# A gated cross-attention and expert layer: the router's logits computed as extra columns of the projection

## The chip, the cores and the metric

The kernel runs on one core of one Trainium2 chip. TensorE (PE) multiplies matrices, VectorE (DVE) and ScalarE (ACT) do elementwise work, GpSimd (POOL) does small operations and issues the indirect transfers, SyncE (SP) issues most of the plain ones. The metric is the device time of one execution in microseconds, the median of several runs. All data are float32.

## The reference

A cross-attention of 4096 rows on 3202 context rows, gated by a tanh and added to x; then a layer norm, a router with eight experts (two per row, at most 640 rows per expert), and the experts' two matrix products, gated and added again.

```python
def xattn(encoder_hc, decoder_hq, w_sim, b_sim, W_qv, b_qv):      # (4096, 512), (3202, 512)
    w1, w2, w3 = w_sim[:d], w_sim[d:2*d], w_sim[2*d:]
    Sim = (encoder_hc @ w1)[:, :, None] + (decoder_hq @ w2)[:, None, :] \
        + einsum('bid,bjd->bij', encoder_hc * w3, decoder_hq) + b_sim[0]
    A = softmax(Sim, axis=2)
    hq_hat = einsum('bij,bjd->bid', A, decoder_hq)
    Batt = softmax(max(Sim, axis=2), axis=1)
    hc_bar = einsum('bi,bid->bd', Batt, encoder_hc)[:, None, :]
    hc_hat = broadcast_to(hc_bar, encoder_hc.shape)
    feats = concatenate([encoder_hc, hq_hat, encoder_hc * hq_hat, encoder_hc * hc_hat], axis=-1)
    return feats @ W_qv + b_qv                                    # W_qv (2048, 512)

def ffn(xf, w_router, b_router, w1, b1, w2, b2):                  # E = 8 experts, top 2, FF = 2048
    logits = xf @ w_router + b_router
    gates = softmax(logits, axis=-1)
    topv, topi = top_k(gates, 2)
    cap = int(1.25 * n / e)                                       # 640 slots per expert
    ...
    h = gelu(einsum('ecd,edf->ecf', buf, w1) + b1[:, None, :])
    out = einsum('ecf,efd->ecd', h, w2) + b2[:, None, :]
    ...

x = x + tanh(g_xattn[0]) * xattn(layernorm(x), ctx_1024, ...)
x = x + tanh(g_ffn[0]) * ffn(layernorm(x), ...)
```

Two facts of this computation matter for the change. The logits are a product of the normed row with the router: with mean m and standard deviation s of a row x1, ((x1 - m) / s) @ w_router equals (x1 @ C) / s, where C is w_router with each column's mean taken away, since a constant row times C gives zero. And x1 itself is a sum of x, a bias and products with the four blocks of W_qv, so x1 @ C can be had by multiplying the same factors with (block @ C).

## The kernel before

The kernel has three stages.

Stage 1 (L112 to L720) works through the 4096 rows in eight groups of 512. `stage_s` computes the scores of a group against all context rows; `stage_e` subtracts each row's maximum (L433), exponentiates on ScalarE (L434) and sums; `stage_v` multiplies by the context's values (L493) and forms the factors of the projection. `stage_d` (L616 to L672) of the group before follows `stage_s`: it multiplies hq_hat and x * hq_hat with the second and third block of W_qv. Each of these products is done with seven half-size products in place of eight, from sums and differences of the quarters (names such as A11, S1, p6, u2, u3 are those of that scheme). In `stage_d` a product `prod` (L631) has two row blocks of 128 by four contraction chunks, each a matmul with 256 columns, and both row blocks share one PSUM bank; VectorE sums them (L646, L656, L660), scales by 1/sum and adds x and the bias (L642), and the rows go to DRAM as `r_d` (L672). A ring of six PSUM banks (`ps_m`) serves scores, values and projection.

Group 0 differs: it also builds what the later groups read. `build` (L251) makes the combined keys, `build_values` (L284) and `build_weights` (L288 to L301) the combined values and the combined projection weights, which go through the double-buffered tiles vc and vs to the DRAM tensors kt_d, vs_d and wt_d. The maximum of group 0 passes through transposes (mps, L405) and a product with ones (mbps) before `stage_e`, and the values products of group 0 are the plain ones (vv).

Stage 2 (L738 to L953) goes over the rows again, in tiles of 128. Its steps hold four tiles (seven steps) or two (the last two). For every tile, `tile_mm` (L780) multiplies q with the weights W1 + hc * W4 (x1p, L792; four matmuls of 512 columns), adds r (L796) to get x1, stores it to `out` (L797), and takes its statistics (L799, L800). `norms` (L803) computes rstd on GpSimd (L806, L807) and the normed rows xn on VectorE (L810). `tile_tr` (L814) transposes xn with four matmuls against the identity (helper line L99) and copies them to SBUF on ScalarE (L817); `tile_logits` (L820) multiplies with the router in four matmuls of 8 columns and adds its bias (L824). `route` (L826) does the top 2 on small VectorE operations, counts slots with two matmuls against a triangle and ones (L881, L882), and `slots` writes weights (L902), token number (L906) and slot (L916) behind each normed row. `dispatch` (L921) then scatters a step's rows to their experts' buffer `buf_d` with two indirect transfers per tile, issued by GpSimd (L924). The tile xn has three buffers, so that step k writes into what the scatters of step k - 3 read.

The loop at the end of stage 2 sets the order: step g's `tile_mm` and `norms`, then the scatters of step g - 2 with `slots`, then transposes, logits and routing of step g - 1. A scheduler then moves instructions that are ready on each engine. The loads of q (q2T, L784), of r (L789) and of the first expert's weights (L731, L733) are on SP's queue; those weights are placed after the q2T loads of groups 1 and 3.

Stage 3 (L961 to L1176) runs the experts. Its first load from buf_d (xb, L1027) needs all scatters.

Of the kernel before, what the change touches and what calls it, by code (L numbers as in the profile page):

```python
# [14 lines left out]
P = 128  # L15
# [5 lines left out]
def gated_layer(ctx, tc, x, x_t, ctxt, ctxt_t, g_xattn, g_ffn, w_sim, w_sim1, b_sim, W_qv, b_qv, w_router, b_router, w1, b1, w2, b2, out):  # L21
# [13 lines left out]
    TG = 4 * P  # L35
    NG = N // TG
# [24 lines left out]
    tgx = const.tile([P, 1], F32, name="tgx")  # L61
    nc.scalar.activation(tgx, gx, AF.Tanh)
    tgf = const.tile([P, 1], F32, name="tgf")
# [3 lines left out]
    r_d = [dram.tile([P, D], F32, name=f"r_d{t}", tag=f"r_d{t}") for t in range(NT)]  # L67
# [8 lines left out]
    tok_i = const.tile([P, NT], I32, name="tok_i")  # L76
# [3 lines left out]
    sno_i = const.tile([P, E * NST], I32, name="sno_i")  # L80
    nc.gpsimd.iota(sno_i, pattern=[[P, E * NST]], base=0, channel_multiplier=1)
    sno = const.tile([P, E * NST], F32, name="sno")
    nc.vector.tensor_copy(sno, sno_i)

    def layernorm(sm, dst, src, t):
        st = sm.tile([P, 6], F32, name=f"st{t}", tag="st")
        nc.vector.bn_stats(st, src)
        mv = sm.tile([P, 2], F32, name=f"mv{t}", tag="mv")
        nc.vector.bn_aggr(mv, st)
        rstd = sm.tile([P, 1], F32, name=f"rstd{t}", tag="rstd")  # L90
        nc.gpsimd.tensor_scalar(rstd, mv[:, 1:2], EPS, None, ALU.add)
        nc.gpsimd.tensor_tensor(rstd, rstd, neghalf, ALU.pow)
        return nc.vector.tensor_scalar(dst, src, mv[:, 0:1], rstd, ALU.subtract, ALU.mult)
# [18 lines left out]
    with ExitStack() as s1:  # L112
# [16 lines left out]
        wt_d = dram.tile([P, 4, DC, 256], F32, name="wt_d", tag="wt_d")  # L129
# [6 lines left out]
        def diag_rows(dst, name, col):  # L136

            dg = sb.tile([P, 4, P], F32, name=f"dg{name}", tag="dg")
            tt(dg, ident.unsqueeze(1).to_broadcast([P, 4, P]), col.unsqueeze(2).to_broadcast([P, 4, P]), ALU.mult)
            nc.tensor.matmul(dst, ones, dg.rearrange("p a b -> p (a b)"), start=True, stop=True)  # L140
# [51 lines left out]
        def stage_a_rest(qs):  # L192
# [4 lines left out]
            ts(bqv, bqv, tgx, None, ALU.mult)  # L197

        def stage_n(g):
# [16 lines left out]
            nc.gpsimd.tensor_scalar(mr[:, 1, :], mv[:, :, 1], EPS, None, ALU.add)  # L216
            nc.gpsimd.tensor_tensor(mr[:, 1, :], mr[:, 1, :], neghalf.to_broadcast([P, 4]), ALU.pow)
            nc.gpsimd.tensor_copy(mr[:, 0, :], mv[:, :, 0])
            nc.gpsimd.dma_start(mr_d[g].rearrange("k i p -> p k i"), mr)
            nc.gpsimd.dma_start(mrb, row_of(mr_d[g]))  # L220
            for i, q in enumerate(qs):
# [66 lines left out]
        def build_weights(c):  # L288


            vc = sb.tile([P, 2, D], F32, name=f"wc{c}", tag="vc", bufs=2)
            for h in range(2):
                with tc.issue_after(queue[-1].ins):
                    nc.sync.dma_start(vc[:, h, :], W_qv[(h + 1) * D + c * P : (h + 1) * D + (c + 1) * P, :])
            B11, B12, B21, B22 = (vc[:, h, k : k + 256] for h in range(2) for k in (0, 256))
            wt = sb.tile([P, 4, 256], F32, name=f"wt{c}", tag="vs", bufs=2)
# [4 lines left out]
            nc.scalar.dma_start(wt_d[:, :, c, :], wt)  # L301
# [59 lines left out]
        def stage_s(g):  # L361
# [8 lines left out]
            for jj, js in enumerate(PAIRS):  # L370
# [29 lines left out]
                else:  # L400
                    for h in (1, 0):
                        tt(m, m, e[:w, :, h], ALU.max)  # L402
            ps = ps_tr.tile([P, 4, P], F32, name=f"mps{g}", tag="tr")
            for i in range(4):
                nc.tensor.transpose(ps[:, i, :], M[:, i // 2, 0, (i % 2) * P : (i % 2 + 1) * P], ident)  # L405
# [3 lines left out]
            diag_rows(ps, f"m{g}", mt)  # L409
# [11 lines left out]
            live[g]["mt"], live[g]["mb"] = mt, mb  # L421

# [58 lines left out]
        def stage_v(g, early, between):  # L481
# [17 lines left out]
            if g == 0:  # L499
                for i in range(2):  # L500
# [86 lines left out]
            v["x"] = []  # L587
            for i in range(4):
                t = 4 * g + i
                xr = sb.tile([P, D], F32, name=f"xr{t}", tag="xr", bufs=4)  # L590
                with tc.issue_after(queue[-1].ins):
                    nc.sync.dma_start(xr, x[t * P : (t + 1) * P, :])
                with tc.issue_after(v["last"].ins):
                    tt(xr, xr, bqv, ALU.add)
                v["x"].append(xr)
# [20 lines left out]
        def stage_d(g):  # L616
            v = live.pop(g)
            A, xs, ri = v["A"], v["x"], v["ri"]

            def prod(ps, p, start=True, stop=True):  # L620
                wt = st.tile([P, DC, 256], F32, name=f"wp{g}_{p}", tag="st")
                natural = {"1": (0, 0), "2": (1, 0), "3": (1, 256)}
                if p in natural:
                    h, c = natural[p]
                    src = W_qv[(h + 1) * D : (h + 2) * D, c : c + 256].rearrange("(k p) d -> p k d", p=P)
                else:
                    src = wt_d[:, {"5": 0, "6": 1, "7": 2, "4": 3}[p], :, :]
                nc.sync.dma_start(wt, src)
                for m in range(2):
                    for k in range(DC):  # L630
                        nc.tensor.matmul(  # L631
                            ps[:, m, :], A[p][:, k, m * P : (m + 1) * P], wt[:, k, :],
                            start=start and m == 0 and k == 0, stop=stop and k == DC - 1, skip_group_check=True,
                        )

            def tmp(k):
                return sb.tile([P, 2, 256], F32, name=f"{k}d{g}", tag=k)

            def out(c, i, j):
                for m in range(2):  # L640
                    r = xs[2 * i + m][:, j * 256 : (j + 1) * 256]
                    stt(r, c[:, m, :], ri[:, 2 * i + m : 2 * i + m + 1], r, ALU.mult, ALU.add)  # L642

            def out_sum(ps, u, i, j):
                c = tmp("p1")
                tt(c, ps, u, ALU.add)  # L646
                out(c, i, j)

            pa = bank(f"pad{g}")
            prod(pa, "1", stop=False)  # L650
            p1 = tmp("p1")
            nc.scalar.copy(p1, pa)
            p6 = bank(f"p6d{g}")
            prod(p6, "6")
            u2 = tmp("u2")
            tt(u2, p6, p1, ALU.add)  # L656
            p7 = bank(f"p7d{g}")
            prod(p7, "7")
            u3 = tmp("u3")
            tt(u3, p7, u2, ALU.add)  # L660
            pb = bank(f"pbd{g}")
# [4 lines left out]
            p4 = bank(f"p4d{g}")  # L666
# [4 lines left out]
            for i in range(4):  # L671
                nc.sync.dma_start(r_d[4 * g + i], xs[i])  # L672


        zero = kv.tile([P, R], F32, name="zero")
        nc.gpsimd.memset(zero, 0.0)
        nc.gpsimd.memset(zero[:, D + 2 : D + 3], float(4 * N))
# [4 lines left out]
        for g in range(NG):  # L682
# [9 lines left out]
            def between():  # L692
# [6 lines left out]
                if g:  # L699
                    for _ in range(-(-E * NST // (NG - 1))):  # L700
                        if blocks:
                            i = blocks.pop()
                            with tc.issue_after(queue[-1].ins):
                                nc.sync.dma_start(buf_d[i * P : (i + 1) * P, :], zero)
# [9 lines left out]
        hs = sm.tile([P, NG, DC + 1], F32, name="hs", tag="hs", bufs=1)  # L714
# [23 lines left out]
    with ExitStack() as s2:  # L738
# [4 lines left out]
        ps_tr = s2.enter_context(tc.tile_pool(name="ps_tr2", bufs=2, space=PSUM, reuse_waits="tile"))  # L743
        ps_lg = s2.enter_context(tc.tile_pool(name="ps_lg", bufs=2, space=PSUM, reuse_waits="tile"))
        ps_po = s2.enter_context(tc.tile_pool(name="ps_po", bufs=1, space=PSUM, reuse_waits="tile"))

        W1 = c2.tile([P, DC, D], F32, name="W1")
        W4 = c2.tile([P, DC, D], F32, name="W4")
        nc.sync.dma_start(W1, W_qv[0:D, :].rearrange("(c p) d -> p c d", p=P))
        nc.sync.dma_start(W4, W_qv[3 * D : 4 * D, :].rearrange("(c p) d -> p c d", p=P))  # L750
        for c in range(DC):
            nc.vector.scalar_tensor_tensor(
                W1[:, c, :], W4[:, c, :], hc[:, c : c + 1], W1[:, c, :], ALU.mult, ALU.add
            )
        wr = c2.tile([P, DC, E], F32, name="wr")
        nc.sync.dma_start(wr, w_router.rearrange("(c p) e -> p c e", p=P))
# [12 lines left out]
        st2 = {}  # L769
# [10 lines left out]
        def tile_mm(t, mv):  # L780
            g, i = divmod(t, 4)
            if g not in qTs:
                qTs[g] = sb.tile([P, DC, TG], F32, name=f"q2T{g}", tag="q2T")
                ld = nc.sync.dma_start(qTs[g], qT_d[g])  # L784
                if g in (1, 3):
                    with tc.issue_after(ld.ins):
                        load_half(0, g // 2)
            r = sb.tile([P, D], F32, name=f"r2_{t}", tag="r2")
            nc.sync.dma_start(r, r_d[t])  # L789
            ps = ps_mm.tile([P, D], F32, name=f"x1p{t}", tag="mm")  # L790
            for c in range(DC):
                nc.tensor.matmul(  # L792
                    ps, qTs[g][:, c, i * P : (i + 1) * P], W1[:, c, :], start=(c == 0), stop=(c == DC - 1)
                )
            x1 = sb.tile([P, D], F32, name=f"x1_{t}", tag="x1", bufs=G + 2)
            nc.vector.scalar_tensor_tensor(x1, ps, tgx, r, ALU.mult, ALU.add)  # L796
            nc.scalar.dma_start(out[t * P : (t + 1) * P, :], x1)  # L797
            st = sm.tile([P, 6], F32, name=f"st{t}", tag="st")
            nc.vector.bn_stats(st, x1)  # L799
            nc.vector.bn_aggr(mv[:, t - STEPS[step_of[t]][0], :], st)  # L800
            return x1

        def norms(k, x1s, mv):  # L803
# [3 lines left out]
            nc.gpsimd.tensor_tensor(rstd, rstd, neghalf.to_broadcast([P, n]), ALU.pow)  # L807
            xg[k] = sb.tile([P, G, R], F32, name=f"xn{k}", tag="xn")
            for i, x1 in enumerate(x1s):
                nc.vector.tensor_scalar(  # L810
                    xg[k][:, i, :D], x1, mv[:, i, 0:1], rstd[:, i : i + 1], ALU.subtract, ALU.mult
                )

        def tile_tr(t):  # L814
            ps = transposed(ps_tr, xg[step_of[t]][:, t - STEPS[step_of[t]][0], :D], f"xps{t}")
            xT = sb.tile([P, DC, P], F32, name=f"xT{t}", tag="xT")
            nc.scalar.copy(xT, ps)  # L817
            st2[t] = xT

        def tile_logits(t, lg):  # L820
            ps = ps_lg.tile([P, E], F32, name=f"lgp{t}", tag="lg")
            for c in range(DC):
                nc.tensor.matmul(ps, st2[t][:, c, :], wr[:, c, :], start=(c == 0), stop=(c == DC - 1))
            nc.vector.tensor_tensor(lg[:, t - STEPS[step_of[t]][0], :], ps, br, ALU.add)  # L824
# [112 lines left out]
        half_routed = None  # L937
        for g in range(len(STEPS) + 1):
            if g < len(STEPS):
                mv = sm.tile([P, G, 2], F32, name=f"mv{g}", tag="mv")  # L940
                norms(g, [tile_mm(t, mv) for t in STEPS[g]], mv)
            if half_routed is not None:
                dispatch(g - 2, half_routed())
            if g >= 1:
                lg = sm.tile([P, G, E], F32, name=f"lg{g}", tag="lg", bufs=2)
                tiles = STEPS[g - 1]
                for i, t in enumerate(tiles):
# [282 lines left out]
```

## Time and profile before

| | us |
|---|---|
| three runs | 2739.01, 2740.75, 2742.1 (median 2740.75) |
| the profiled execution | 2740.97 |
| its span in the profile | 2739.2 |
| end of the last projection product of stage 1 | 1515.2 |
| first matmul of x1p | 1519.63 |
| first scatter of steps 0, 1, 2, 3, 4 | 1578.0, 1603.7, 1626.0, 1648.3, 1671.1 |
| last scatter's end | 1725.9 |
| first product of an expert | 1734.0 |

The span runs from the first to the last instruction of one profiled execution, and 1.8 us lie around it. The granted TensorE clock was 0.986 on average.

A row of a group of instructions reads: line, engine, operation, output <- inputs, shapes, count; then the busy time and the mean length of one in ns; then the idle time of the engine just before these instructions and what ended it. One float32 matmul appears as two instructions of TensorE. In a row of the timeline, the start and the length in us come first, and the brackets hold the idle time before it and its releaser.

### The profile page before, as it was taken

How to read it: one execution, taken by the hardware profiler on the slowest of the kernel's cores; microseconds unless marked ns; L12 is line 12 of the kernel's file. 1: busy time of each engine (PE TensorE's matmuls, PEld its weight loads, DVE VectorE, ACT ScalarE, POOL GpSimd, SP SyncE). 2: the span in 40 equal slices, each digit the busy share in tenths (PEclk: the TensorE clock that was granted, in tenths of full speed). 3: DMA queues.
4: the chain of work that ended last, by engine and by line, in shares of the span. 5: the costliest groups of instructions: out<-in, count | busy, mean ns of one | idle time of the engine just before them, and what ended most of it. 6: DMA issues, size and time to landing. Idle time of an engine off the chain costs nothing. (4 is left out here: it accounts for less than half of the span.)

```text
span 2739.2 us, 29771 instructions
## 1 busy us (share of the span) xinstructions
PE 2662.6 (97%) x11368; PEld 2101.5 (77%) x11368; DVE 1694.0 (62%) x3318; ACT 412.5 (15%) x665; POOL 218.5 (8%) x257
## 2 busy tenths in 40 slices
PE   8999999999999999999999997799999999999998
PEld 7548888888888888888888554477777777777776
DVE  7765946847558468376583556655747465755654
ACT  1200201202002012021020011111111211111111
POOL 0100000000000000000000045201010010101010
PEclk9999999999999999999999998899999999999999
DMA  7786646646656467466454863222233231423210
GB/s 281 196 294 177 216 158 175 233 162 165 228 161 217 166 167 232 155 171 226 154 187 144 317 230 109 91 77 100 93 118 110 81 123 63 152 81 105 81 58 20
DMA packets 183234, 429.54 MB, mean 157 GB/s; under 512 B 17607, under 2 KB 80320, under 8 KB 181044
## 3 DMA queue, kind: packets, MB, share of 16 engines
q1 hardware_dynamic: 152226, 353.64, 39.9%
q0 software_dynamic: 13648, 36.55, 4.0%
q10 hardware_dynamic: 17217, 37.44, 3.6%
q8 instruction: 90, 1.47, 0.2%
q14 instruction: 53, 0.43, 0.0%
HBM read 351.43 MB, written 83.30 MB: 159 GB/s over the span
## 5 line engine op out<-in xcount | busy, mean ns | idle before, releaser
L384 PE MATMUL pas<-Qp,kt 128*128 128x256 f32 (+1 forms) x728 | 174.6, 381 | 1.2 <-ACT p1s L341 1.2
L994 PE MATMUL pah<-bT,w 128*128 128x320 f32 x512 | 159.0, 433 | 0.9 <-DVE cf L1040 0.8
L493 PE MATMUL pbv<-E,vt 128*128 128x256 f32 (+1 forms) x728 | 159.5, 379 | 0.0
L384 PEld LDWEIGHTS pas<-Qp,kt 128*128 128x128 f32 (+1 forms) x728 | 135.6, 187 | 22.8 <-ACT p1s L341 1.6
L493 PEld LDWEIGHTS pbv<-E,vt 128*128 128x128 f32 (+1 forms) x728 | 138.3, 190 | 18.8
L434 ACT ACTIVATE E<-E 128x1024 f32<-128x1024 f32 (+1 forms) x112 | 110.7, 995 | 167.6 <-DVE E L433 166.2
L433 DVE TENSOR_TENSOR E<-E,mb 128x1024 f32<-128x1024 f32 (+1 forms) x112 | 125.4, 1139 | 12.4 <-ACT mb L420 12.4
L994 PEld LDWEIGHTS pah<-bT,w 128*128 128x128 f32 x512 | 97.1, 190 | 39.9 <-DVE bT L1035 1.2
L792 PE MATMUL x1p<-W,q2T 128*128 128x512 f32 x256 | 122.6, 627 | 4.4 <-DMA q2T<-qT_d 4.4
L994 PE MATMUL pao<-w,h 128*128 128x256 f32 x512 | 121.0, 379 | 0.0
L1146 PE MATMUL op<-w,h 128*128 128x512 f32 x256 | 113.6, 592 | 0.0
L402 DVE TENSOR_TENSOR M<-M,E 128x1024 f32<-128x1024 f32 (+1 forms) x96 | 109.0, 1135 | 6.4
L1169 POOL DMA_INDIRECT out<-acc,ti x40 | 42.8, 1071 | 854.5 <-DVE acc L1168 854.2
L994 PEld LDWEIGHTS pao<-w,h 128*128 128x128 f32 x512 | 96.8, 190 | 16.6 <-issue 4.3
L341 ACT COPY p1s<-pas 128x512 f32<-128x512 f32 (+1 forms) x56 | 31.1, 555 | 488.3 <-issue 257.0
L357 DVE TENSOR_TENSOR E<-p4s,u3s 128x512 f32<-128x512 f32 (+1 forms) x56 | 36.5, 651 | 106.8 <-PE p4s L384 106.8
L792 PEld LDWEIGHTS x1p<-W,q2T 128*128 128x128 f32 x256 | 49.2, 201 | 56.8 <-issue 56.8
L384 PE MATMUL pbs<-Qp,kt 128*128 128x256 f32 (+1 forms) x364 | 88.5, 385 | 4.0 <-DVE E L352 4.0
L445 DVE TENSOR_TENSOR SM<-SM,E 128x1024 f32<-128x1024 f32 (+1 forms) x80 | 88.6, 1107 | 0.0
L1146 PEld LDWEIGHTS op<-w,h 128*128 128x128 f32 x256 | 47.2, 190 | 52.0 <-issue 46.4
L384 PE MATMUL pbs<-q,kt 128*128 128x256 f32 (+1 forms) x364 | 86.6, 379 | 0.0
L384 PE MATMUL p6s<-q,kt 128*128 128x256 f32 (+1 forms) x364 | 86.6, 379 | 0.0
(390 smaller groups left out, 5253.0 us busy)
## 6 DMA issues: line engine op xcount, KB each, us to landing
kt<-kt_d SPq DMA_DIRECT2D x84, 896.0 KB
w<-in_w SPq DMA_DIRECT2D x32, 2048.0 KB
vt<-vs_d SPq DMA_DIRECT2D x28, 896.0 KB
vt<-vs_d SPq DMA_DIRECT2D x28, 640.0 KB
wp<-wt_d SPq DMA_DIRECT2D x32, 512.0 KB
wp<-in_W_qv SPq DMA_DIRECT2D x24, 512.0 KB
kt_d<-ktb ACTq DMA_DIRECT2D x12, 896.0 KB
buf_d<-zero SPq DMA_DIRECT2D x40, 258.0 KB
```

The lines of the kernel that those rows point to most:

```text
L341: nc.scalar.copy(p1, cut(pa))
L357: tt(done(1, 0), cut(p4), u3, ALU.add)
L384: nc.tensor.matmul(ps[:w, jl, :], kts[j][:, KSLOT[p], k, :], B[p][:, k, :], start=start and jl == 0 and k == 0, stop=stop and k == 1, skip ...
L402: tt(m, m, e[:w, :, h], ALU.max)
L433: live[g]["last"] = tt(e, e, m, ALU.subtract)
L434: live[g]["exp"] = nc.scalar.activation(e, e, AF.Exp)
L445: tt(s, E_t[0][:, lr] if jj == 1 else s, e, ALU.add)
L493: nc.tensor.matmul(ps[b], vt[: WJ[j], j - i * JH, b * P : (b + 1) * P], right(j), start=start and j == 0 and (b == 0 or g == 0), stop=stop ...
L792: nc.tensor.matmul(ps, qTs[g][:, c, i * P : (i + 1) * P], W1[:, c, :], start=(c == 0), stop=(c == DC - 1))
L994: nc.tensor.matmul(ps, a, b, start=start and i == 0, stop=stop and i == len(A) - 1, skip_group_check=True)
L1146: nc.tensor.matmul(ps, hT[:, k, 2 * MH :], W2[:, k, :], start=(k == 0), stop=(k == KH - 1))
L1169: sc = nc.gpsimd.indirect_dma_start(out=out[:, :], out_offset=rows_of(ti, s), in_=acc[:, :], in_offset=None, bounds_check=N - 1, oob_is_er ...
```

## The change

The normed row is no longer transposed and multiplied with the router. Instead, the centred router C (`wrc`) is multiplied with the blocks of W_qv once, in group 0 (`router_weights`, 64 matmuls of 8 columns, reading a transposed copy of W_qv), and the results `we` stand as extra columns beside the weights: four columns in each of the two halves of the projection's products of `stage_d` (260 columns in place of 256, BW), and eight in each half of x1p's weights (264, B1), where the second half's extra columns hold C itself, for the part of x1 that is x. The rows r_d carry four extra columns per half. What `tile_mm` has after a tile are x1 and, with two small VectorE operations, its unnormed logits; `norms` multiplies them by rstd and adds the bias.

What comes from the second half's columns is q @ C, and q is the layer norm of x, so it is multiplied with the standard deviation `sd` of x, which is kept from stage 1. The row norm (xn) moves from VectorE to ScalarE as scale and bias. [...]each product of `stage_d` has two banks, and its sums on VectorE are split in two; x1p has two banks per tile. `build_weights` now also stores the plain quarters of the weights to wt_d (with the extra columns), so that all weights of `stage_d` are read from there. The first expert's weights are placed after the q2T loads of groups 3 and 6. Some tiles share memory (tok_i, tgx, tgf, hs), and the zero block is stored in two halves.

```diff
-    r_d = [dram.tile([P, D], F32, name=f"r_d{t}", tag=f"r_d{t}") for t in range(NT)]
+    r_d = [dram.tile([P, 2, BW], F32, name=f"r_d{t}", tag=f"r_d{t}") for t in range(NT)]
...
+            for c in range(DC):
+                nc.tensor.matmul(ps, ones, wrc[:, c, :], start=c == 0, stop=c == DC - 1)
+            mean = be
+            ts(mean, ps, 1.0 / D, None, ALU.mult)
+            tt(wrc, wrc, mean.unsqueeze(1).to_broadcast([P, DC, E]), ALU.subtract)
...
+        def router_weights():
...
+            for k, pieces in enumerate(parts):
+                for a, f0, n in pieces:
+                    with tc.issue_after(queue[-1].ins):
+                        nc.sync.dma_start(a, W_qv_t[:, :, k * D + f0 : k * D + f0 + n])
+            def step(ks):
+                for k in ks:
+                    for a, f0, n in parts[k]:
+                        for f in range(n // P):
+                            for d in range(DC):
+                                nc.tensor.matmul(
+                                    ps[:, k, (f0 // P) + f, :], a[:, d, f * P : (f + 1) * P], wrc[:, d, :],
...
+            return step, lambda: nc.vector.tensor_copy(we, ps)
...
-            wt = sb.tile([P, 4, 256], F32, name=f"wt{c}", tag="vs", bufs=2)
+            nc.vector.tensor_copy(vc[:, :, :, 256:], we[:, 1:3, c, :].rearrange("p h (j e) -> p h j e", j=2))
+            nc.scalar.dma_start(wt_d[:, 0:4, c, :], vc.rearrange("p h j d -> p (h j) d"))
+            wt = sb.tile([P, 4, BW], F32, name=f"wt{c}", tag="vs", bufs=2)
...
+            if g == 0:
+                rw, rw_end = router_weights()
+                rw([0])
             ps = ps_tr.tile([P, 4, P], F32, name=f"mps{g}", tag="tr")
...
+            def banks(name):
+                return [bank(f"{name}d{g}_{m}").rearrange("p a b -> p (a b)")[:, :BW] for m in range(2)]
             def prod(ps, p, start=True, stop=True):
-                wt = st.tile([P, DC, 256], F32, name=f"wp{g}_{p}", tag="st")
+                wt = st.tile([P, DC, BW], F32, name=f"wp{g}_{p}", tag="st")
+                nc.sync.dma_start(wt, wt_d[:, slot[p], :, :])
                 for m in range(2):
                     for k in range(DC):
                         nc.tensor.matmul(
-                            ps[:, m, :], A[p][:, k, m * P : (m + 1) * P], wt[:, k, :],
+                            ps[m], A[p][:, k, m * P : (m + 1) * P], wt[:, k, :],
...
+            def total(dst, ps, u):
+                for m in range(2):
+                    tt(dst[:, m, :], ps[m], u[:, m, :], ALU.add)
+                return dst
...
-            ps = ps_mm.tile([P, D], F32, name=f"x1p{t}", tag="mm")
-            for c in range(DC):
-                nc.tensor.matmul(
-                    ps, qTs[g][:, c, i * P : (i + 1) * P], W1[:, c, :], start=(c == 0), stop=(c == DC - 1)
-                )
+            ps = ps_mm.tile([P, 2, 512], F32, name=f"x1p{t}", tag="mm")
+            for j in range(2):
+                for c in range(DC):
+                    nc.tensor.matmul(
+                        ps[:, j, :B1], qTs[g][:, c, i * P : (i + 1) * P], W1[:, c, j, :], start=(c == 0), stop=(c == DC - 1)
+                    )
...
+            nc.vector.scalar_tensor_tensor(
+                l_.rearrange("p (j e) -> p j e", j=2), ps[:, 0, 256:B1].rearrange("p (j e) -> p j e", j=2), tgx,
+                r[:, :, 256:], ALU.mult, ALU.add,
+            )
+            nc.vector.scalar_tensor_tensor(l_, ps[:, 1, 256:B1], sd[:, t : t + 1], l_, ALU.mult, ALU.add)
...
+            nc.vector.tensor_tensor(l_, l_, rstd.unsqueeze(2).to_broadcast([P, n, E]), ALU.mult)
+            nc.vector.tensor_tensor(l_, l_, br.unsqueeze(1).to_broadcast([P, n, E]), ALU.add)
+            nc.vector.scalar_tensor_tensor(nb, mv[:, :n, 0], -1.0, rstd, ALU.mult, ALU.mult)
             for i, x1 in enumerate(x1s):
-                nc.vector.tensor_scalar(
-                    xg[k][:, i, :D], x1, mv[:, i, 0:1], rstd[:, i : i + 1], ALU.subtract, ALU.mult
-                )
+                nc.scalar.activation(
+                    xg[k][:, i, :D], x1, AF.Identity, scale=rstd[:, i : i + 1], bias=nb[:, i : i + 1]
+                )
-        def tile_tr(t):
...
-        def tile_logits(t, lg):
...
```

## The prediction, made before the changed kernel ran

> **What bounds the kernel now.** I read the page first, for the engine that is busy and the places where it is not.
>
> ```profile
> PE 2662.6 (97%) x11368; PEld 2101.5 (77%) x11368; DVE 1694.0 (62%) x3318; ACT 412.5 (15%) x665; POOL 218.5 (8%) x257
> PE   8999999999999999999999997799999999999998
> POOL 0100000000000000000000045201010010101010
> PEclk9999999999999999999999998899999999999999
> ```
>
> TensorE bounds the whole run: 97% busy. In the 40 slices (68.5 us each) it falls to 7 only in slices 24 and 25, 1643 to 1780 us, just where GpSimd is busy. So I cut stage 2 into stretches of 20 us (busy PE, PEld, DVE, ACT, POOL, then clock, DMA share, GB/s).
>
> ```profile
> 1600.00:1620.00 20.00, 20.00 (x68) 11.70 (x68) 10.65 (x50) 1.65 (x4) 8.23 (x10) 0.82 0.67 232
> 1620.00:1640.00 20.00, 19.44 (x85) 11.55 (x84) 11.58 (x55) 1.74 (x4) 8.87 (x9) 1.00 0.63 217
> 1680.00:1700.00 20.00, 11.58 (x58) 7.36 (x56) 11.94 (x81) 2.71 (x6) 10.82 (x13) 0.89 0.18 62
> 1700.00:1720.00 20.00, 7.47 (x32) 6.91 (x32) 12.81 (x84) 1.39 (x3) 12.65 (x12) 0.50 0.04 9
> ```
>
> PE looks full until 1680, but a modelled matmul end covers short waits. The waits and the timeline of stage 2 say more; first two lines of the waits (us in total, times, longest), then GpSimd's and VectorE's timeline.
>
> ```profile
> DVE xn L906 <- DMA buf_d<-xn,sidx: 20.3, 4, 7.2
> PEld lgp L823 <- ACT xT L817: 17.0, 17, 3.9
> ```
> ```profile
> 1626.01 1.08 POOL L924 DMA_INDIRECT buf_d<-xn,sidx  x1 [5.06 <-DVE d L842]
> ...
> 1635.09 0.97 POOL L924 DMA_INDIRECT buf_d<-xn,sidx  x1 [0.30 <-issue]
> 1641.93 0.22 POOL L806 TENSOR_SCALAR rstd<-mv 128x4 f32<-128x4 f32 x1 [5.87 <-DVE tmp L890]
> 1648.34 1.08 POOL L924 DMA_INDIRECT buf_d<-xn,sidx  x1 [5.06 <-DVE d L842]
> ```
> ```profile
> 1640.01 0.17 DVE L906 COPY xn<-tok 128x4 f32<-128x4 f32 x1 [5.52 <-DMA buf_d<-xn,sidx]
> 1643.32 1.92 DVE L810 TENSOR_SCALAR xn<-x,mv,rstd 128x512 f32<-128x512 f32 x4 [1.16 <-POOL rstd L807]
> ```
>
> That is a loop. Eight scatters take 10.05 us; 3.95 us after the last one VectorE's copy of token numbers into the reused xn buffer (three buffers) may run; VectorE stands until then with everything behind it; then the step's last tile, rstd on GpSimd, four normalisations, slots; 8.33 us after the copy the next scatters start. 10.05 + 3.95 + 8.33 = 22.33 us, the distance of the two scatter groups. From step 1 on this loop, not PE, sets stage 2's pace; four laps have the DMA wait.
>
> The groups of stage 2 and of group 0, for the prices:
>
> ```profile
> L792 PE MATMUL x1p<-W,q2T 128*128 128x512 f32 x256 | 122.6, 627 | 4.4 <-DMA q2T<-qT_d 4.4
> L823 PE MATMUL lgp<-wr,xT 128*128 128x8 f32 x256 | 34.6, 266 | 9.2 <-ACT xT L817 6.2 <-DVE pos L889 3.0
> L817 ACT COPY xT<-xps 128x512 f32<-128x512 f32 x32 | 18.2, 586 | 148.5 <-DMA q2T<-qT_d 56.6 <-PE xps L99 43.4 <-DVE tmp L888 20.9
> L631 PE MATMUL pbd<-wp,hs 128*128 128x256 f32 x256 | 57.9, 379 | 0.0
> PE pbs L384 <- DVE E L352: 4.0, 1, 4.0
> L493 PE MATMUL vv<-E,vt_(0_0)_0_803 128*128 128x512 f32 x28 | 14.4, 678 | 3.0 <-ACT E L434 3.0
> ```
>
> A mean is latency, not pace: counts of the timeline give the pace. One f32 matmul is two instructions; 64 of 512 columns take 30.43 us with a cold start, 0.43 each warm (0.84 ns per column), 256 columns 0.216 us, and eight router matmul instructions of N=8 take 0.95 us (0.119 each), eight transposes 1.07.
>
> **What the Trainium skill says.** "PSUM — Partial Sum Buffer", The four PSUM rules: a matmul's output must fit one bank, 512 f32 columns. Two halves of 260 do not, so every product of the projection and every x1p tile now takes two banks; no run of before shows what this costs. "DMA: Bandwidth & Descriptors", Anatomy of one DMA: about 2 us of a transfer are fixed, mostly the receipt of the write. Here 3.95 us pass from the end of the last scatter's row to the copy, so the loop's landing term is larger than the page says and stays as measured. "TensorE: Matmul & The Clock Gate", The HAM clock gate: an idle array falls to half clock until some 3.4 us of work; the 0.50 at 1700 to 1720 agrees.
>
> **The change part by part.** Signs: plus is slower. Profiled run 2740.97 us, span 2739.2; the median of the three runs is 2740.75, so differences carry over unchanged.
>
> (1) Stage 2 up to the first scatters. The fourth tile of step 2 ends PE's stretch before rstd(2), which stands ahead of scatters(0) on GpSimd. Before, x1p starts at 1519.63 and rstd(2) at 1570.85, 51.2 later: 6.2 first tile + 11 x 3.44, + four transpose and router sets of step 0 (4 x 2.02 = 8.1), less overlap. After, the sets are gone and a tile has 16 instructions of 264 columns, 3.565 us: 6.2 + 11 x 3.565 + 2.4 (x, statistics) = 47.8. From rstd(2) to the scatters 7.15 us before; without four xn (1.84) and with two logits operations instead of four waits on PE I take 5.2. First scatter 53.0 after t0 instead of 58.4: -5.4.
>
> (2) The laps. In the changed instruction order the same copy (now L1002) stands in the same place with the same wait on the scatters, so the loop remains. From copy to scatters: 3.45 us (copy, last tile's x and its two small logit operations, statistics, 1.3 of rstd) + 28 small operations at 0.107 and one x of 0.67 = 3.7, + 0.25: 7.4 instead of 8.33. The xn normalisation goes to ScalarE, 15% busy: four of about 0.6 (the L817 row's 586 for 512 columns) beside the routing; if that cover failed, 2.4 us a step. A lap is 10.05 + 4.15 (3.95 to 4.3) + 7.4 = 21.6. From sc0 to sc1 26 us before (PE too had to finish), 22.7 now, then three laps of 22.3 to 22.7 become 21.6. sc4 begins 140.7 instead of 151.4 after t0: -10.7 including (1). Without the loop PE would need 4 x 3.565 = 14.3 us a step and VectorE some 16.5; so most of what PE gives back goes into waiting for scatters.
>
> (3) The tail, sc4 to the last scatter's end: 54.8 us before. After: group 5 follows by 10.05 + 1.3 rstd + 0.9 routing = 12.2, group 6 by 11.7, the rest (16 scatters) 20.5 back to back, 2.5 for the expert-weight sums sharing VectorE: 46.9, -7.9. Stage 2 in all -18.6; the tail leans on every cover holding, so I take -17, bounds -12 and -21.
>
> (4) Queues: SP issues three r_d stores instead of two ahead of q2T, and q2T is awaited already (4.45 us): +1.2. The loads of the first expert's weights (2 MB each) move from before tile 4 and tile 10 to after r of tiles 6, 9, 18 and 20; r is loaded three tiles (10.7 us) ahead, and 2 MB at the 350 to 400 GB/s of that stretch is 5.5 us, so nothing waits; the last is there long before 1717, when it is first read.
>
> (5) Projection in stage 1: 8 groups x 7 products x 16 instructions = 896 of 260 instead of 256 columns, 4 x 0.84 ns = 3.4 ns each: +3.0, all on PE. Five bank reads are now two operations each, some 1 us more VectorE per group; slack there is 2 to 10 us per group around the sums. One ScalarE copy in two. Ring of six banks: the fourth product must wait for VectorE's u2 of the second. If VectorE is on time, nothing; else see the rivals. Bounds 0 and +2 us a group, I take 0.
>
> (6) Group 0. 64 router-weight matmuls of N=8, 128 instructions x 0.119 = 15.2 us, put around the maximum's transposes. PE idles there in before (1.5 + 1.5 us and the 3.0 of the vv row, half clock after), so only about 5.7 us reach the first values product. The build chain of values and weights on VectorE with DMA-held buffers runs until about 203, and PE waits for its end at 212.6 (the 4.0 line). It begins about 2.3 later, and vc is now held by a store too (four stores of 532 KB added): 2 to 5. Taken +6, bounds +3 and +14. Eight more matmuls for the means: +0.7. The 4 MB of W_qv_t come behind the key loads, landing before they are read; if not, up to +5.
>
> (7) Twelve half-size zero stores a group instead of six, an extra GpSimd multiply, aliased tiles: the zero stores are issued in SP gaps and GpSimd is 8% busy; 0, at worst 1.
>
> Sum: -17 + 1.2 + 3.0 + 6 + 0.7 + 0 = -6.1: 2740.75 - 6.1 = 2734.7 us.
>
> **Rivals.** (A) As summed, 2734.7 us. (B) The copy's wait doesn't bind, because it is taken late enough or the scatters land in 2 us: four laps at 17 (VectorE's 16.5 and a little) instead of 21.6, -19: 2716. Against it: the order keeps the copy's wait. For it: VectorE's operations ahead of the copy are fewer, so its place in time may differ. (C) Group 0 eats it: +12 in place of +6, 2741; for it, VectorE's chain there already waits for DMA in turns, and stores are added. (D) Slower: the projection's two banks per product. The fourth product's first bank waits for the second product's sum on VectorE, which at that time is subtracting maxima from the scores (1139 ns each) in every group; it decides once that sum comes over 3.5 us (one product, 16 x 0.219) after its product ends. A wait of 2 us in each of eight groups is +16: 2751. For it: the six-bank ring has no spare bank in the changed order; against it: in before no sum of that stage was shown late. That the change does not remove the work is excluded: the instruction order has no transpose or router matmul on the rows.
>
> **How the numbers follow.** Chances: A 0.42, B 0.17, C 0.14, D 0.27. A measurement of this kernel tells about 0.2%, 5.5 us, from no change. A's own spread (2727 to 2741, from the bounds of 3 and 6) lies two thirds beyond that: 0.28 faster, 0.14 same. Faster 0.28 + 0.17 = 0.45, same 0.14 + 0.14 = 0.28, slower 0.27. Range 2715 to 2754: from B to a little beyond D, A's own range 2727 to 2741.
>
> **What would show it.** Scatter groups 21.6 us apart and L1002 waiting on the scatters' DMA: (2) right; 17 us apart: B. First scatter 53 us after the first x1p: (1). PE's first wait in group 1 about 6 us later: (6); by 12: C. A row of PE waits in the projection's fourth product on VectorE: D. I am wrong also if ScalarE's xn delays the exponentials behind it.

## The result, and the profile after

In the first series the changed kernel took 2751.08 us (median of six runs, 2746.63 to 2753.73), the kernel before 2741.77: a ratio of 1.0033 with an interval of 1.002 to 1.0046, slower where 2734.7 was forecast. Two later series put the kernel before at 2750.4 and 2749.2 us and the changed one at 2748.8 and 2748.3 (ratios 0.9997 and 0.9998). So the change is worth between nothing and a loss of 0.33%; it is not the gain of 0.22% that was forecast. The time came from two large pieces of opposite sign:

| mark, us | before | after | shift |
|---|---|---|---|
| group 0's scores end, TensorE | 95.6 | 101.5 | +5.9 |
| first values product (vv) | 104.3 | 128.7 | +24.4 |
| rsps, behind group 0's last values product | 195.8 | 220.9 | +25.1 |
| first product of the projection | 283.5 | 306.3 | +22.8 |
| first x1p | 1519.6 | 1545.05 | +25.4 |
| last scatter's end | 1725.9 | 1733.4 | +7.5 |
| first transpose of stage 3 | 1730.0 | 1737.7 | +7.7 |
| span | 2739.2 | 2749.1 | +9.9 |

Stage 2, from the first x1p to stage 3's first transpose, went from 210.4 to 192.7 us: -17.7. Group 0 took 25 us more. Stage 3, which the change leaves alone, took 2.2 us more in this pair; over all traces of this document it takes 1009.2 to 1014.8 us. The rows of the page that showed a full TensorE before:

```profile
PE 2656.2 (97%) x11384; PEld 2139.7 (78%) x11384; DVE 1689.9 (61%) x3410; ACT 420.0 (15%) x673; POOL 219.8 (8%) x268
PE   8999999999999999999999985699999999999998
POOL 0000000000001000000000035201010010101010
PEclk9799999999999999999999998899999999999999
```

TensorE looks as busy as before, and in stage 2 even less so (8, 5, 6 where 9, 7, 7 stood). The one new thing is a 7 in the second slice of the granted clock, 69 to 137 us: group 0. The timeline of TensorE there, first before, then after:

```profile
97.06 0.66 PE L405 MATMUL mps<-ident,M 128*128 128x128 f32 x4 [1.50 <-DVE M L402]
99.22 2.07 PE L140 MATMUL mbps<-dgm,ones 128*128 128x512 f32 x2 [1.51 <-DMA vt_(1_0)_0_879<-in_ctxt]
104.31 14.39 PE L493 MATMUL vv<-E,vt_(0_0)_0_803 128*128 128x512 f32 x28 [3.02 <-ACT E L434]
```
```profile
100.43 1.03 PE L448 MATMUL pbs<-Qp,ktb 128*65 128x256 f32 x4
101.29 4.62 PE L249 MATMUL we<-wrc,wq 128*128 128x8 f32 x32
105.76 1.09 PE L472 MATMUL mps<-ident,M 128*128 128x128 f32 x4
106.65 6.83 PE L249 MATMUL we<-wrc,wq 128*128 128x8 f32 x32
113.33 2.05 PE L155 MATMUL mbps<-dgm,ones 128*128 128x512 f32 x2
115.18 13.66 PE L249 MATMUL we<-wrc,wq 128*128 128x8 f32 x64
128.69 15.11 PE L568 MATMUL vv<-E,vt_(0_0)_0_918 128*128 128x512 f32 x28
```

The 128 instructions of the router-weight matmuls (we, L249), called the row from here on, take 25.1 us. The first 32 take 0.144 us each, the others 0.213. The clock beside them, in stretches of 5 us (columns as before, the clock third from the end):

```profile
95.00:100.00 5.00, 5.00 (x25) 3.18 (x24) 4.18 (x7) 0.60 (x2) 0.61 (x1) 1.00 0.99 167
100.00:105.00 5.00, 5.00 (x36) 4.58 (x34) 2.12 (x4) 0.14 (x1) 0.00 (x0) 0.87 1.06 345
105.00:110.00 5.00, 5.00 (x26) 5.00 (x25) 1.67 (x4) 0.00 (x0) 0.38 (x1) 0.50 1.06 344
120.00:125.00 5.00, 5.00 (x25) 5.00 (x24) 5.00 (x6) 4.75 (x7) 0.95 (x1) 0.50 0.95 307
```

From 105 to 110 us TensorE and its weight loads both show as busy all the time, and yet the clock is at 0.50. By the mean of 0.87 from 100 to 105 us (3.7 us at 1.00 and 1.3 at 0.50, an estimate) it fell some 2.4 us into the row; in a second trace of the changed kernel (e4_after, 0.85 there) the same sum gives 5. It is back at 1.00 from 135 us, some 6 us into the values products.

In stage 2 the loop is still there, at the line it has now, and TensorE has new waits of 12.4 and 20.9 us for VectorE behind it:

```profile
DVE xn L1002 <- DMA buf_d<-xn,sidx: 35.1, 5, 11.0
```
```profile
PE pos L977 <- DVE mask L967: 20.9, 2, 11.5
PE x1p L885 <- DVE mv L903: 12.4, 3, 6.6
```

The first scatters of steps 0 to 7 start at 1598.5, 1622.4, 1646.8, 1666.9, 1687.2, 1699.8, 1712.0 and 1722.5 us. A lap, from one step's first scatter to the next step's, takes 23.8, 24.5, 20.0 and 20.4 us for the first four.

### The profile page after: what moved, and what is told of

It is laid out like the page before. It is cut to its first block, busy times and chain, and to the rows that moved or that the text cites. A ratio compares the mean times of both kernels' runs of the same rounds, so it can differ in the third digit from the quotient of the medians.

```text
span 2749.1 us, 29996 instructions
## 1 busy us (share of the span) xinstructions
PE 2656.2 (97%) x11384; PEld 2139.7 (78%) x11384; DVE 1689.9 (61%) x3410; ACT 420.0 (15%) x673; POOL 219.8 (8%) x268
## 5 line engine op out<-in xcount | busy, mean ns | idle before, releaser
L885 PE MATMUL x1p<-W,q2T 128*128 128x264 f32 x512 | 126.6, 411 | 18.9 <-DVE mv L903 12.4
L885 PEld LDWEIGHTS x1p<-W,q2T 128*128 128x128 f32 x512 | 103.3, 204 | 39.9 <-issue 20.8
```

The source lines that it names most:

```text
L885: nc.tensor.matmul(ps[:, j, :B1], qTs[g][:, c, i * P : (i + 1) * P], W1[:, c, j, :], start=(c == 0), stop=(c == DC - 1))
```

## The experiments

Every series has its own runs of the kernel before on the same chip, and ratios are to those. The four series of this section ran on four different chips.

**A wider moving operand (e1_pad64).** Why did the row run at half clock? The edit gives the same matmuls more columns, zeros that add nothing:

```diff
+        WZ = 64
...
+            wrz = sb.tile([P, DC, WZ], F32, name="wrz", tag="ebb")
+            nc.gpsimd.memset(wrz, 0.0)
+            nc.vector.tensor_copy(wrz[:, :, :E], wrc)
...
-                                    ps[:, k, (f0 // P) + f, :], a[:, d, f * P : (f + 1) * P], wrc[:, d, :],
+                                    pw[:, (k * DC + f0 // P + f) * E : (k * DC + f0 // P + f) * E + WZ],
+                                    a[:, d, f * P : (f + 1) * P], wrz[:, d, :],
```

> The changed kernel, but the 64 router-weight matmuls of group 0 have 64 columns instead of 8, of which 56 are zeros that are added to neighbouring results; the same 128 weight loads. Theory 1 (a row of 8-column matmuls streams too little to hold TensorE's clock, which falls to 0.50 and doubles every weight load): the clock stays near 1.0 from 101 to 117 us, the row takes about 128 x 0.119 = 15 us instead of 25, the first values product starts about 11 us earlier than 128.7, the kernel needs about 2740 us instead of 2751. Theory 2 (the clock falls for another reason, the pauses around it or the transfers beside it): no change, 2751 us. Theory 3 (columns cost): slower by 128 x 56 x 0.84 ns = 6 us at most.

Measured: 2735.44 us, ratio 0.9979 (0.9969 to 0.9989), 15 us below the changed kernel and below the kernel before. The twenty runs form two groups, ten from 2726.3 to 2733.3 us and ten from 2737.6 to 2743.0; the trace is of the lower group, and all lie below the lowest run of the changed kernel in any series, 2744.6. The row in its timeline, and the clock:

```profile
99.29 3.68 PE L256 MATMUL we<-wrz,wq 128*128 128x64 f32 x32
...
103.25 3.68 PE L256 MATMUL we<-wrz,wq 128*128 128x64 f32 x32
106.77 1.08 PE L155 MATMUL mbps<-dgm,ones 128*128 128x512 f32 x2
107.68 7.25 PE L256 MATMUL we<-wrz,wq 128*128 128x64 f32 x64
114.77 12.24 PE L576 MATMUL vv<-E,vt_(0_0)_0_921 128*128 128x512 f32 x28
```
```profile
105.00:110.00 5.00, 5.00 (x42) 4.52 (x41) 1.65 (x3) 0.82 (x2) 0.38 (x1) 1.00 1.07 355
110.00:115.00 5.00, 5.00 (x46) 5.00 (x45) 5.00 (x5) 4.69 (x5) 0.36 (x1) 1.00 1.09 352
```

With eight times the columns the row takes 14.6 us instead of 25.1 (0.114 an instruction), at the full clock, and the values products after it start warm (12.24 for 28 instructions against 15.11). The transfers are as heavy as before (DMA share 1.07), so they are not the cause.

**Sixteen columns (e2_pad16)**, the same edit with 16 for 64.

> As the run with 64 columns, with 16 columns (8 of them zeros). If the clock falls because the array streams for too small a part of the time, 16 columns, about 27 of each 119 ns by the 0.84 ns per column and two instructions, should still be too few: the row takes 20 to 25 us and the kernel 2745 to 2751 us. If anything but the 8-column form itself holds the clock, 2735 us.

Measured: ratio 1.0008 (1.0001 to 1.0015). The row, and the clock in one of its stretches:

```profile
99.01 3.64 PE L256 MATMUL we<-wrz,wq 128*128 128x16 f32 x32
...
110.59 13.67 PE L256 MATMUL we<-wrz,wq 128*128 128x16 f32 x64
```
```profile
110.00:115.00 5.00, 5.00 (x23) 4.48 (x22) 3.55 (x4) 2.72 (x4) 0.46 (x1) 0.50 1.08 341
```

The row takes 23.3 us; its last 64 instructions are as slow as with 8 columns. So more than 16 columns per 128-column weight load are needed here, and 64 are enough; where between them the bound lies was not looked for. (At 0.84 ns per column, 16 columns are about 13 of the 119 ns of one instruction, not 27: the expectation set two instructions against the time of one. 64 are about 54.)

**Three quarters of the row left out (e1_skip)**, the start and stop flags set to match.

```diff
-                            for d in range(DC):
+                            for d in range(1):
                                 nc.tensor.matmul(
...
```

> The changed kernel with 16 of the 64 router-weight matmuls of group 0: three of the four terms of each sum over the contraction are left out. It prices the row with everything else in place. If group 0's row is what the prediction under-priced, the first values product starts some 17 to 20 us earlier (48 matmuls = 96 instructions at 0.2 us) and the kernel takes about 2732 us. If the build chain of values and weights or the stores to DRAM bind behind it, much less comes out at the end, 2740 us or more.

Measured: 2742.1 us, ratio 0.9999 (0.999 to 1.0008): 9 us less than the changed kernel, not 19. The values products start at 108.3 and end 21.4 us earlier (199.7), but the first x1p comes only 12.0 earlier. Between them, TensorE's timeline in group 1's scores, VectorE's last builds, and ScalarE behind them (ACTq is its issue of a store):

```profile
217.84 3.68 PE L448 MATMUL pas<-Qp,kt 128*128 128x256 f32 x8 [10.38 <-ACT p1s L405]
```
```profile
195.16 0.43 DVE L339 TENSOR_TENSOR vsv<-vcv 128x256 f32<-128x256 f32 x1 [5.63 <-DMA vs_d<-vsv]
...
213.35 0.43 DVE L361 TENSOR_TENSOR wt<-wc 128x260 f32<-128x260 f32 x1 [6.41 <-DMA wc<-in_W_qv]
...
215.36 0.42 DVE L364 TENSOR_TENSOR wt<-wc,wt 128x260 f32<-128x260 f32 x1
```
```profile
215.82 0.37 ACTq L365 DMA_DIRECT2D wt_d<-wt  x1
216.22 1.07 ACT L591 COPY hqT<-vv 128x512 f32<-128x512 f32 x2 [43.57 <-DMA kt<-kt_d]
217.18 0.60 ACT L405 COPY p1s<-pas 128x512 f32<-128x512 f32 x1
```

The chain of builds, links that wait in turns for loads and stores of two buffers, ends at 215.8, 16 us behind the last values product. ScalarE issues the store of the last build, then makes its copies, and TensorE waits for the second of them. The same chain stands in the other traces:

| us | before | after | e1_skip | e1_pad64 |
|---|---|---|---|---|
| product mbps starts | 99.2 | 113.3 | 103.1 | 106.8 |
| chain, first build starts | 121.8 | 133.3 | 126.1 | 125.8 |
| VectorE's idle time in the chain | 29.8 | 42.2 | 38.6 | 31.7 |
| chain, last build ends | 202.7 | 226.6 | 215.8 | 208.4 |
| rsps, behind the last values product | 195.8 | 220.9 | 199.5 | 204.1 |
| first product of the projection | 283.5 | 306.3 | 293.8 | 286.5 |

In all 16 traces that have the builds in group 0, those of the kernel before among them, the projection starts 78.0 to 81.1 us after the chain's end; after rsps it is anything from 79.5 to 94.3. So the chain, and not the values products, decides when group 1 goes on (in e2_pad64_xn4 the two end together), and the row's delay reaches the end through it. The chain starts behind VectorE's subtraction of the maxima, which needs mbps, and the first half of the row stands ahead of mbps. In the changed kernel it starts 11.5 us later than before and lasts 12.3 longer (93.2 instead of 80.9), and all of that length is idle time. It lasts 78.0 to 84.7 us in the five such traces with 64 columns and 89.7 to 96.0 in the eight with 8 or 16, this one included; the added stores are in all thirteen. What makes the difference was not settled. That the chain also splits the runs of e1_pad64 in two groups is possible and not shown.

**The column means later (e1_centre_late).** The block that computes them becomes a function called behind the third score chain.

> The changed kernel, but the eight instructions for the router's column means come after the third score chain instead of at 19 us, just after the start. Theory 1: the scores of the first chain no longer run at half clock (3.8 us for eight instructions became 2.0), group 0's scores end about 4.5 to 5 us earlier, the kernel takes about 2746 us. If the slow start has another cause (the later first row, the extra loads), the scores end at 101 us as before and the time is 2751 us.

Measured: 2748.92 us, 1.0032 (1.0022 to 1.0041): no change that can be told. The scores end at 99.7. Other runs of the unmoved block end them at 98.5 to 101.7, so the changed kernel's first trace was the late end of a spread, and the block's place isn't the cause. The first row of score products still runs cold (3.49 us for eight instructions against 1.99) and starts 1.1 us later than before. The kernel before does not always run it warm either: in its second trace (e4_before) these eight take 3.78 us and the scores end at 97.2.

**The first expert's weights earlier (e1_weights_early)**, `if g in (1, 3)` for `(3, 6)`.

> The changed kernel with the first expert's weights placed after the loads of q of groups 1 and 3, as in the kernel before. If the long first two laps of the scatters (23.8 and 24.5 us against 20.0 and 20.4 later) come from these 2 MB loads on the same transfer engines (landing 6.1 and 6.8 us against 2.3 and 2.7), the laps fall to about 21 us and the kernel gains 4 to 7 us, 2745 us. If they come from something else, or if the weights then delay the first tiles' rows by as much, 2751 us.

Measured: 2748.58 us, 1.0026 (1.0016 to 1.0035); laps of 24.3, 24.1, 20.4 and 21.0. My expectation fell: with the last of these loads issued at 1577.6, it is still 6.6 us from the end of step 0's last scatter (1604.0) to VectorE's copy. The transfer engines are at a share of 1.0 from 1590 to 1606 even so. Which transfers fill them was not separated.

**The builds of the projection's weights moved into group 1 (e2_pad64_late)**, on top of the 64 columns.

```diff
+                if g == 1 and 1 <= jj <= 4:
+                    with tc.issue_after(e_add.ins):
+                        build_weights(jj - 1)
...
-                        with tc.issue_after(v["last"].ins):
-                            build_weights(2 * i + h)
```

> As the run with 64-column router-weight matmuls (2735 us), and the four builds of the projection's combined weights move out of group 0's chain of builds into the scores of group 1, one behind each score chain. The chain of builds (82 us, two buffers, each link a transfer to DRAM) holds VectorE past the end of group 0's values product, and TensorE waits for it. If it binds, the chain ends some 15 us earlier, the waits of TensorE at the start of group 1's scores go away and the kernel takes about 2731 us. If that wait is only a first-product wait that any group 1 has, no change, 2735 us; if the moved builds hold up VectorE between the score chains, slower, 2740 us.

Measured: 0.9974 (0.9965 to 0.9983), which is not to be told from 0.9979. The wait of 2.6 us at the start of group 1 went, but another came, where ScalarE's copy stands behind the issue of a store of these builds:

```profile
280.73 3.64 PE L456 MATMUL pas<-Qp,kt 128*128 128x256 f32 x8 [5.99 <-ACT p1s L413]
```

**The row norm back on VectorE (e2_xn_dve)**, the four lines of `norms` as before.

> The changed kernel with the row norm xn back on VectorE (four operations of 0.54 us per step). It splits stage 2's gain of 17.7 us. If the loop of scatters, landing, copy and VectorE's operations sets the pace, as predicted, each of seven steps gets up to 1.8 us longer and the kernel takes 2751 + 8 to 12 us. If the gain came from TensorE's removed work alone, no change, 2751 us.

Measured: 1.0007 (0.9998 to 1.0015); the changed kernel has 1.0033, 0.9997 and 0.9998 in three other series. Stage 2 takes 192.2 us against 192.7. The move to ScalarE is worth nothing that shows here. VectorE is busy for 15.3 us more (1705.2 us), but its wait for the scatters, now in front of the norm, is 21.5 us shorter than the 35.1 of the changed kernel:

```profile
DVE xn L918 <- DMA buf_d<-xn,sidx: 13.6, 4, 6.1
```

By these two numbers the norm fits into time in which VectorE otherwise stands.

**Four buffers for xn**, `bufs=4` in `norms`: on the changed kernel with 64 columns (e2_pad64_xn4), and on the kernel before alone (e3_before_xn4).

> As the run with 64 columns, with four buffers for xn in place of three, so that the copy of token numbers waits for the scatters of one step earlier. If the copy's wait for the landing sets the laps (20 to 24.5 us), they fall towards VectorE's work and the scatters' own 10 us + rstd, 16.5 to 18 us, and the kernel takes about 2735 - 15 = 2720 us; stage 2 then ends later by the last scatters only. If GpSimd's scatters or VectorE's work bind anyway, 2730 to 2735 us.

> The kernel before with a fourth buffer for xn and nothing else. If its stage 2 is set by the loop through three buffers, as the prediction read it (22.3 us a lap against about 19.4 us that TensorE's own work would need), three or four laps lose some 3 us each and it gains 8 to 12 us, 0.3 to 0.4%. If TensorE's transposes and router matmuls bound it after all, no change.

Measured: 0.9912 (0.9893 to 0.9931) and 0.9948 (0.9929 to 0.9966). Stage 2 falls from 193.6 (e1_pad64) to 185.4 us in the first, to 202.0 from 210.4 in the second. So the buffer loop bound both kernels. In the changed one the laps became 23.0, 23.9, 19.4 and 17.4, from 24.2, 24.9, 20.0 and 20.6: only the fourth came into the expected 16.5 to 18, and stage 2 gave 8.2 of the expected 15 us. VectorE's wait for the scatters halved, from 36.2 us:

```profile
DVE xn L1010 <- DMA buf_d<-xn,sidx: 17.5, 4, 7.4
```

In the second the whole gain is 15 us, more than the 8.4 of stage 2 (10.7 against e4_before); where the rest lies is open, since no trace of the kernel before comes from that chip.

**Together, and the changed kernel again.**

> The changed kernel once more, as an anchor beside the others of this series: a ratio of 1.0033 to the kernel before (interval so far 1.002 to 1.0046). If the run with xn on VectorE (1.0007) was really 0.26% faster than the changed kernel, this one must lie well above 1.0015; if the two are the same kernel in time, it lies near 1.0007 to 1.002.

> The changed kernel with the three edits together: 64-column router-weight matmuls, four buffers for xn, and the builds of the projection's weights moved into group 1's scores. The first two alone gave a ratio of 0.991; the third gave nothing measurable by itself. Expected 0.990 to 0.991, about 25 us below the kernel before.

> The changed kernel with 64-column router-weight matmuls, four buffers for xn, and the row norm back on VectorE. With the buffer wait eased, VectorE's work is nearer to the bound of a lap (about 12 of 20 us busy before), so four times 0.54 us a step should cost 5 to 12 us against 0.991 if it binds; if it is covered by the scatters, nothing, 0.991.

Measured: 0.9997 (0.9989 to 1.0006), 0.9937 (0.9921 to 0.9954) and 0.9883 (0.9867 to 0.99). The late builds add nothing that can be told: without them it was 0.9912, with an interval that overlaps. The changed kernel's ratio moved because the kernel before took 2750.4 us in this series. Where that lies, the next series shows:

> The kernel before once more, with a trace of its own from this series. The median of the kernel before was 2741.8, 2746.1 and 2750.4 us in three series, that of the changed kernel 2751.1 and 2748.8. Theory: stage 1 is the same to 1 us (first x1p at 1519 to 1521 us), and the difference lies in stage 2's laps, in the landing of the scatters: stage 2 of the kernel before, 210.4 us in the first trace, takes up to 219 us where it takes 2750 us. Rival: the difference is spread over the whole run (clock), and all marks shift in proportion.

> The changed kernel in the same series. If its stage 2 depends less on the landing, its time stays at 2748 to 2751 us and the ratio goes with the kernel before: about 1.003 where that one takes 2742 us, 1.000 where it takes 2750 us.

> 64-column router-weight matmuls and four xn buffers, row norm on ScalarE, beside the same with the norm on VectorE, so that the two stand in one series (so far 0.991 and 0.988 in two series). If the place of the norm matters at all, they differ by more than 0.2%; if not, both lie at the same ratio.

> The same with the norm on VectorE: 0.9867 to 0.99 of the kernel before as measured in the last series, 2715 to 2720 us.

Measured: the kernel before 2749.28 us (1.0), the changed one 0.9998 (0.999 to 1.0007), the two others 0.9923 (0.9901 to 0.9945) and 0.9902 (0.988 to 0.9924). In this trace the kernel before is later by 2.1 us at the first x1p, by another 2.4 in stage 2 and by 1.3 in stage 3: neither stage 2 alone nor one place. Since the series ran on different chips, the chip may be what moves it; no run separates the two. Against this trace the changed kernel stands +18.8 at the first x1p and -20.0 in stage 2; its row of router-weight matmuls takes 23.1 us here. So the two pieces are there in both series with traces of both kernels, and their difference is what moves. In time the norm's place can't be told apart at 0.2%. In the traces with four buffers stage 2 is shorter with the norm on VectorE (181.0 and 182.3 us against 184.8 to 185.5 in three traces with it on ScalarE), and the first lap is 18.4 us in both, against 22.4 to 23.0.

The best version measured is the changed kernel with 64 columns, four xn buffers and the norm on VectorE: 2717.26 and 2722.84 us, 0.988 and 0.990 of the kernel before.

## Why the prediction was wrong

- Step (1), right: 53.0 us from the first x1p to the first scatter, measured 53.5.
- Step (2), right in its sum, by luck: sc4 at 140.7 (its own parts add up to 140.5), measured 142.2. From copy to scatters it took 7.6 where 7.4 was forecast, but the laps were not 21.6 each. The landing, taken as 4.15, was 6.1 and 6.8 us in the first two laps and 2.3 and 2.7 in the next two, and these errors nearly cancel. The xn move was counted as part of the shortening from copy to scatters, and no gain from it shows.
- Step (3), right: 46.9 us for the tail, measured 46.2. Stage 2 in all: forecast -17, measured -17.7.
- Step (4): +1.2 for the wait for q2T, measured +0.8. The weights' loads at nothing: moved back, they changed nothing that can be told.
- Step (5), right in its mechanism, a little high: +3.0, measured +1.8 from the first product of the projection to the last. Seven groups took 0.35 each longer; the last took 0.6 less, and its 0.72 us wait for ScalarE's copy (p1d, L652 before) is gone. No wait for the two banks per product appears, so rival D's mechanism is out; that its time, 2751, is what came is luck.
- Step (6), the one that failed: "64 router-weight matmuls of N=8, 128 instructions x 0.119 = 15.2 us", of which "only about 5.7 us reach the first values product", +6 taken and +14 as the bound. Measured +24.4 there and +22.8 at the projection. The price came from the row of router matmuls in stage 2, where they stand between products of 512 columns. In a row of their own they ran at half clock and cost 25.1 us; with 64 columns, at full clock, 14.6. The hiding was judged about right: from the scores' end to the first values product it was 8.7 us before, with 6.0 of it idle, 27.2 after, with none, and 15.3 with 64 columns. So at the forecast price 6.6 us reach the values product, at the real one 18.5. The eight matmuls for the means, +0.7, stand for a later end of the scores by 5.9 in this pair and 1.3 in the pair of the last series.
- Step (6) did name the chain of builds, which is what the projection waits for, but set its start about 2.3 us later and its cost at 2 to 5. It began 11.5 us later and ended 23.9 later.
- The sum: up to the first product of the projection +6.7 was forecast and +22.8 came; from there to the first x1p +4.2 and +2.6; in stage 2 -17 and -17.7; in stage 3 nothing and +2.2. That is -6.1 forecast, +9.9 in the traces.
- Rival C named the place. Its +12 was half of what came. Its reason, a chain of builds that waits in turns, is part of it; its stores are not what made it long, since with them and 64 columns the chain of e1_pad64 takes 82.6 us against 80.9 before.
- Rival B, laps of 17 us with the copy's wait gone, is not what the change does, but what a fourth buffer does in part.

## What to carry to other kernels

A price from a row in one place holds only with its neighbours: ask what keeps the clock up where the instructions will stand. Here small matmuls moved out of a stream of large ones went from 0.119 us to as much as 0.213 each, and more columns of zeros made them faster. Ask also which chain of work the next stage waits for: a delay counts by what it does to that chain, not by the engine it stands on. A loop through reused buffers and transfers binds although every engine looks free; count its laps before crediting work that is taken off an engine, and try one buffer more.

## What the runs showed of the hardware that I had not expected

- A row of float32 matmuls with 8 or 16 columns, each with a 128-column weight load, lets the granted clock fall from 1.00 to 0.50 although TensorE and its weight loads show as 100% busy; with 64 columns it stays at 1.00 (0.213 against 0.114 us an instruction). The Trainium skill ("TensorE: Matmul & The Clock Gate", The HAM clock gate) has the array warm after one busy window; here the array lost the full clock in a stretch that the profile shows as busy, so the busy share of the profile did not tell whether it stays warm.
- From the end of eight scatters to VectorE's copy it took 2.3 and 2.7 us with a DMA share of 0.48 and 0.31 meanwhile, and 6.1 and 6.8 with 0.70 and 1.03. The skill's some 2 us of fixed cost for one transfer ("DMA: Bandwidth & Descriptors", Anatomy of one DMA) is close to the shortest of these.
